# Four graph layers on one core: new issue times for every step, and the normalisation's shift on GpSimd

## The chip, the cores and the metric

One NeuronCore of a Trainium2 chip runs the program. Its engines are TensorE (PE, matrix products; PEld is its weight load), VectorE (DVE), ScalarE (ACT), GpSimd (POOL) and SyncE (SP), which issues all DMAs here. Each engine runs its own instructions strictly in the order in which the program holds them, and waits on semaphores for the others. The metric is the device time of one execution in microseconds (us); lower is better.

## The reference

64 graphs ("batches") of 256 nodes with 512 features each pass through four layers. Each layer normalises the features, and adds its result to them. All is float32.

```python
h = jnp.maximum(_layernorm(x, axis=-1), 0.0); x = x + L0(h, adj)   # and so for L1, L2, L3
L0: q, k, v = h Wqk, h Wv;  w = softmax_n(sum_m (q k^T / 8) * adj);  w * v
L1: feats = h W (8 heads of 64);  e = leaky_relu(e_self_i + e_neigh_j) masked by A;  relu(softmax(e) feats)
L2: Xp = h Wp; Xc = Xp C^T;  relu(tanh(A * Xc Xp^T) Xp)   (8 heads of 64)
L3: q, k, v = h Wqk, h Wv;  w = softmax_n(sum(q * (adj (k mask))) / sqrt(512));  w * v
```

The layer norm is (x - mean) / sqrt(var + eps), with eps = 1e-5. The kernel computes it as relu(rstd * x + shift), with rstd = (var + eps)^-0.5 and shift = -mean * rstd.

## The kernel before, in words

A batch is a graph of some 150 named steps (`graph`, a function of the kernel); each step issues a few instructions, mostly on one engine. A batch's 256 nodes lie on 128 partitions as two chunks c = 0, 1, so nearly every step works on a tile of 128 partitions by 512 columns or two of them.

The steps of one batch, in the order of the data:

- `load` (SP): x, the adjacency and its 32x32 blocks. `at`, `neg`, `negt`: the transposed adjacency and the masks made from it.
- `normed(layer)`: `st` (bn_stats and bn_aggr, DVE, L690, L692), `rs` (var + eps, DVE, L697), `pw` (power -0.5, POOL, L701), `sh` (the shift, DVE, L706), `hn` (relu(rstd x + shift), ACT, L713), then the transposition of hn into `ht`: `sq` (32x32 transposes, DVE, L645), `sw` (a write of 512 KB to DRAM, SP, L733) and `ht` (four reads back, SP, L650).
- Layer 0: `qk0`, `qk1`, `score0` (PE), `s0v` (DVE), `pv00`, `pv01`, `softp0` (PE), `softv0`, `softw0` (DVE), `softa0` (ACT), `add0` (DVE, L775).
- Layer 1: `fa`, `fb` (features, PE), `fae`, `fbe` (DVE), `send` (DVE), `er` and `enes` (SP: the score rows to DRAM and back to all partitions, 2 MB), `max0` to `max3` (DVE, L896: row maxima), `mxv`, `mxt` (DVE), `mr`, `mb` (SP: the maxima to DRAM and back to all partitions, 1 MB), `ea` (ACT, L935), `eg` (POOL, L942), `eb` (DVE, L948), `ex` (ACT, L954), each for four pairs of heads; `po` (PE, L966), `eh` (POOL, L975: sums over the two chunks), `su`, `sp` (PE), `oe`, `se` (ACT), `sr` (DVE), `sqo`, `swo`, `or` (back through DRAM), `oa0`, `oa1` (POOL, L1032, L1034).
- Layer 2: `xp` (PE), `xe` (DVE), `sqx`, `swx`, `xpt` (through DRAM), `xc` (PE), `xcv`, `xca` (ACT), `ps` (PE, L1097), `tv` (DVE, L1129), `ta` (ACT, L1136), `py` (PE, L1111), `ye` (ACT), `sqy`, `swy`, `yr`, then `yg` (POOL) and `yv` (DVE) add it to x.
- Layer 3: `am` (ACT), `agg` (PE, L1168), `ga` (ACT), `z` (PE), `zv` (DVE), `softp3`, `pv30`, `pv31` (PE), `softv3`, `softa3`, `softw3`, `add3`, `store`.

Matrix products with the full array (fa, fb, qk, pv, xp, z) share the helper `rows` and its line L639; `ps` uses 64 rows of the array, `po` and `py` 64 columns, `su` 32 columns.

**What sets the order.** The tables at the top give every step of a batch a time: `TIMES` for a batch in the steady state, `FIRST` for the first batches (6 of them), `LAST` for the last (5), `WEIGHTS` for the preparation of the weights. `Plan.sequence` adds b * `PERIOD` to the times of batch b and sorts all 9640 steps. The times are only keys: what they set is the order of the instructions on each engine.

```python
steps += [(b * PERIOD + at, b, name) for name, at in times.items()]
return sorted(steps)
```

`Plan.run` issues the steps in this order and ties each instruction to the one before it on its engine, so no scheduler moves them. Some four to five batches are under way at a time. Buffers come from pools in the order of the sequence (`take`, `done`): 8 PSUM banks, 5 `xt`, 3 `ht`, 4 `pair`, 3 `all`, 2 `half`, 2 `sq`, 2 `hn` among them; who takes a buffer waits for the last use of it.

In the steady state the order on four of the queues, from one `pv31` or `add3` to the next (the number in brackets tells batches apart, larger is later), is:

```
PE   pv31(0) qk1(4) qk0(4) pv01(4) score0(4) fb1(3) softp0(4) xp0(2) xp1(2) pv00(4) agg1(1) fb0(3) agg0(1) po2(3) z0(1)
     po0(3) xc(2) po1(3) po3(3) ps0(2) su0(3) fa0(4) fa1(4) su1(3) ps1(2) sp(3) z1(1) py0(2) softp3(1) py1(2) pv30(1)
DVE  add3(0) sh3(1) fbe1(3) xe0(2) softv0(4) sq3(1) xe1(2) sqx(2) softw0(4) eb2(3) add0(4) st1(4) rs1(4) fbe0(3) sh1(4)
     eb0(3) sq1(4) eb1(3) eb3(3) at(5) st0(5) rs0(5) zv0(1) sh0(5) sqo(3) sq0(5) fae0(4) tv1(2) fae1(4) send(4) tv0(2) ...
POOL eh0(0) eh1(0) pw0(2) eh2(0) eh3(0) oa1(0) oa0(0) pw2(0) yg(-1) pw3(-1) eg0(1) eg2(1) eg1(1) pw1(2) eg3(1)
SP   store(0) sw3(1) swx(2) ht3(1) xpt(2) load(5) sw1(4) ht1(4) swo(3) or(3) sw0(5) er(4) enes(4) ht0(5) swy(2) sw2(3) ...
```

Of the kernel before, what the change touches and what calls it, by code (L numbers as in the profile page):

```python
# [9 lines left out]
F32 = mybir.dt.float32  # L10
AF = mybir.ActivationFunctionType
OP = mybir.AluOpType
# [4 lines left out]
P = 128  # L17
# [3 lines left out]
NC = N // P  # L21
# [14 lines left out]
PERIOD = 57.0  # L36
TIMES = {
    "load": 0.000, "at": 0.020, "st0": 0.021, "rs0": 0.040, "pw0": 0.060, "sh0": 0.447, "hn0": 0.467, "sq0": 4.046,
    "neg": 5.196, "sw0": 7.794, "ht0": 17.081, "negt": 24.877, "qk1": 25.097, "qk0": 25.928, "qe0": 26.481,
    "pv01": 26.487, "qe1": 26.501, "score0": 26.521, "s0v": 30.777, "softp0": 30.797, "softv0": 37.191,  # L40
    "softa0": 37.211, "pv00": 41.031, "softw0": 42.595, "add0": 46.118, "st1": 47.198, "rs1": 47.218,
    "pw1": 47.238, "sh1": 48.461, "hn1": 49.969, "sq1": 51.679, "sw1": 57.622, "ht1": 58.705, "fa0": 58.725,
    "fae0": 61.292, "fa1": 62.955, "fae1": 64.080, "send": 64.100, "er": 65.670, "enes": 67.047, "max0": 78.054,
    "max1": 78.465, "max2": 80.041, "ea2": 81.782, "max3": 81.811, "ea0": 82.877, "mxv": 86.226, "fb1": 87.694,
    "mxt": 89.120, "mr": 89.140, "fbe1": 92.928, "mb": 92.952, "ea1": 93.137, "eg0": 97.342, "eg2": 97.898,
    "eb2": 99.758, "fb0": 101.023, "eg1": 102.751, "ex2": 103.007, "fbe0": 104.462, "ea3": 105.281, "eb0": 106.770,
    "po2": 107.965, "ex0": 109.416, "eg3": 110.046, "po0": 110.200, "eb1": 110.242, "ex1": 110.262, "po1": 112.122,
    "eb3": 112.539, "ex3": 112.559, "eh0": 112.721, "po3": 113.362, "eh1": 113.725, "oe0": 113.726, "oe1": 113.772,
    "su0": 114.984, "sqo": 116.823, "swo": 116.843, "or": 116.985, "eh2": 121.455, "eh3": 121.545, "su1": 121.565,
    "se": 121.585, "sp": 124.333, "sr": 124.353, "oa1": 127.236, "oa0": 130.191, "st2": 132.579, "rs2": 132.599,  # L50
    "pw2": 132.619, "sh2": 133.501, "hn2": 135.131, "sq2": 135.151, "sw2": 137.255, "ht2": 140.479, "xp0": 146.490,
    "xp1": 148.494, "xe0": 150.546, "xe1": 153.892, "sqx": 155.064, "swx": 156.419, "xpt": 157.903, "xc": 167.559,
    "xcv": 170.132, "ps0": 171.632, "tv1": 175.365, "xca": 177.302, "ps1": 179.802, "ta1": 179.832, "tv0": 180.487,
    "tv2": 182.563, "ta0": 182.818, "py0": 182.838, "ta2": 182.910, "tv3": 184.557, "ta3": 184.577, "am": 184.723,
    "ye0": 185.950, "py1": 187.683, "ye1": 187.703, "sqy": 190.038, "swy": 190.249, "yr": 195.049, "yv": 200.772,
    "yg": 202.748, "st3": 203.788, "rs3": 205.029, "pw3": 205.049, "sh3": 206.251, "hn3": 206.271, "sq3": 210.021,
    "sw3": 210.041, "agg1": 212.553, "ht3": 213.760, "agg0": 218.026, "ga0": 222.008, "z0": 223.305,
    "zv0": 228.215, "ga1": 230.586, "z1": 239.253, "zv1": 242.471, "softp3": 243.288, "pv30": 245.126,
    "pv31": 252.572, "softv3": 255.150, "softa3": 256.059, "softw3": 260.763, "add3": 262.405, "store": 266.901,
# [3 lines left out]
    "wn0": 268.900, "wqk": 269.000, "mt0": 269.100, "mv0": 270.100, "mm0": 270.300, "wn1": 270.400, "mt1": 271.100,  # L63
    "wv0": 271.800, "wa": 271.900, "w11": 272.400, "mv1": 272.700, "sa1": 273.100, "b2": 273.400, "mk": 273.900,
    "wn2": 274.000, "mm1": 274.100, "c2": 274.700, "b1": 274.800, "w10": 275.100, "w13": 275.200, "mt2": 275.300,
    "mv2": 275.400, "w12": 275.700, "sa3": 276.000, "sa0": 276.200, "sa2": 276.800, "mm2": 276.900, "mkp": 278.000,
    "wn3": 278.300, "mt3": 278.900, "mv3": 279.000, "mm3": 279.600, "w21": 279.900, "w22": 281.300, "ma": 281.400,
    "room": 282.600, "w20": 284.300, "mkv": 289.600, "w23": 291.300, "wv3": 295.000,
# [3 lines left out]
        "load": 268.200, "st0": 268.300, "rs0": 268.400, "pw0": 268.500, "at": 268.600, "neg": 268.700,  # L72
        "sh0": 269.200, "hn0": 269.600, "sq0": 269.700, "sw0": 269.800, "ht0": 271.300, "negt": 271.600,
        "qk0": 271.700, "qe0": 272.000, "qk1": 272.100, "qe1": 272.200, "score0": 272.300, "s0v": 272.600,
        "pv00": 273.000, "softp0": 273.200, "softv0": 273.300, "pv01": 273.500, "softa0": 273.600,
        "softw0": 273.700, "add0": 273.800, "st1": 274.200, "rs1": 274.300, "pw1": 274.400, "sh1": 274.500,
        "hn1": 274.600, "sq1": 275.500, "sw1": 276.300, "ht1": 276.500, "fa0": 277.200, "fae0": 277.400,
        "fa1": 277.500, "fae1": 277.600, "send": 277.900, "er": 278.700, "enes": 278.800, "fb0": 279.100,
        "ea2": 279.400, "ea1": 279.500, "fbe0": 280.300, "max0": 280.500, "max1": 280.700, "max3": 280.900,
        "max2": 281.000, "eg1": 281.200, "ea3": 281.600, "ea0": 281.700, "mxv": 281.800, "fb1": 281.900,  # L80
        "fbe1": 282.300, "mxt": 282.400, "eg2": 282.700, "mr": 283.400, "eg3": 283.500, "mb": 283.700,
        "eg0": 284.200, "eb0": 284.800, "eb2": 284.900, "ex0": 285.000, "eb1": 285.100, "po0": 285.200,
        "ex2": 285.300, "eb3": 285.400, "ex1": 285.500, "po2": 285.600, "po1": 285.700, "ex3": 285.800,
        "po3": 285.900, "eh1": 286.100, "eh0": 286.200, "oe0": 286.500, "oe1": 286.600, "su0": 286.800,
        "sqo": 287.200, "swo": 287.300, "or": 287.700, "eh3": 288.000, "eh2": 288.100, "su1": 288.200,
        "se": 288.600, "sp": 288.700, "sr": 288.800, "oa0": 289.700, "oa1": 289.900, "st2": 290.300,
        "rs2": 290.500, "pw2": 290.600, "sh2": 290.700, "hn2": 290.900, "sq2": 291.400, "sw2": 291.800,
        "ht2": 291.900, "xp0": 292.900, "xe0": 293.700, "xp1": 293.900, "xe1": 294.800, "sqx": 294.900,
        "swx": 295.300, "xpt": 295.500, "xc": 297.600, "xcv": 297.800, "xca": 298.200, "ps0": 298.600,
        "tv1": 299.200, "tv0": 299.300, "ta1": 299.700, "ta0": 299.800, "ps1": 299.900, "py0": 300.100,  # L90
        "tv2": 300.200, "tv3": 300.300, "ta2": 300.400, "ta3": 300.500, "ye0": 300.700, "py1": 301.000,
        "ye1": 301.100, "sqy": 301.600, "swy": 304.500, "yr": 304.700, "yg": 304.800, "yv": 305.300,
        "st3": 305.400, "rs3": 306.000, "pw3": 306.100, "sh3": 306.300, "am": 306.700, "hn3": 309.400,
        "sq3": 310.200, "sw3": 310.800, "agg1": 311.300, "agg0": 311.800, "ht3": 312.700, "ga0": 312.900,
        "ga1": 313.200, "z0": 313.800, "zv0": 315.600, "z1": 315.900, "pv31": 316.200, "zv1": 317.100,
        "softp3": 317.200, "pv30": 317.600, "softv3": 318.000, "softa3": 318.400, "softw3": 318.500,
        "add3": 319.000, "store": 319.100,
    },
    {
        "load": 212.500, "st0": 213.200, "rs0": 213.500, "pw0": 213.600, "sh0": 213.700, "hn0": 213.800,  # L100
        "at": 213.900, "sq0": 214.400, "neg": 215.800, "sw0": 215.900, "ht0": 217.900, "qk0": 218.600,
        "qk1": 218.800, "qe0": 218.900, "pv00": 219.100, "qe1": 219.400, "score0": 219.600, "s0v": 219.700,
        "softp0": 220.100, "softv0": 220.300, "softa0": 220.700, "pv01": 220.800, "softw0": 221.100,
        "add0": 221.200, "st1": 221.400, "rs1": 221.500, "pw1": 221.600, "sh1": 222.200, "hn1": 222.300,
        "sq1": 223.000, "sw1": 223.200, "ht1": 224.500, "fa0": 225.200, "fb0": 225.800, "fae0": 225.900,
        "fa1": 226.100, "fbe0": 226.200, "fae1": 229.300, "fb1": 229.400, "send": 229.700, "er": 230.000,
        "negt": 230.600, "enes": 232.800, "ea0": 233.000, "ea2": 233.400, "max0": 233.800, "max2": 234.600,
        "max3": 235.000, "ea3": 235.100, "ea1": 235.200, "max1": 235.300, "mxv": 235.400, "mxt": 235.800,
# [328 lines left out]
def tile_four_gnn_layers(ctx: ExitStack, tc: tile.TileContext, x, adj, nodemask,  # L437
# [48 lines left out]
    far = consts.tile([P, 1], F32)  # L486
    nc.gpsimd.memset(far, NEG_BIG)
    power = consts.tile([P, NC], F32)
    nc.gpsimd.memset(power, -0.5)
    for t in plan.pools["mx"]:  # L490
        nc.gpsimd.memset(t, 0.0)

# [742 lines left out]
```

## Time and profile before

| | us |
|---|---|
| the runs of the kernel | 3867.55, 3868.8, 3875.89 (median 3868.8) |
| the profiled execution, span from the first instruction to the last | 3876.7 |
| PE busy in that span | 3717.5 |
| DVE busy | 3178.4 |
| ACT busy | 1893.0 |
| POOL busy | 1576.0 |

The page gives no time of the profiled execution other than its span. Busy times are sums over an engine's instructions. A row of the timeline has the start in the span, the length, the engine, the line and operation, what it writes and reads (out<-in), the shape and the number of instructions merged into it; brackets at its end give the idle time of the engine before it and who ended that. A float32 matrix product appears as two instructions, and the recorded lengths of PE overlap: the spacing of the starts tells how fast it goes. In the chain of waits each row is a piece of the path that ended last: start, length, what. The row of one line gives the shortest, the median and the longest of its instructions in ns.

### The profile page before, as it was taken

What the parts mean: (1) busy time and instruction counts of PE and PEld (TensorE: products, weight loads), DVE (VectorE), ACT (ScalarE), POOL (GpSimd) and SP (SyncE); (2) the same over time, 40 slices, a digit from 0 to 9 for tenths busy, and PEclk for the clock granted to TensorE, in tenths of its full rate; (3) what the DMA queues carried; (4) which work ended last, traced back from release to release, by engine and by line L of the source; (5) the groups of instructions that cost most, each with busy time, mean ns of one, the idle gap of its engine ahead of it and who ended that gap; (6) DMA issues with size and microseconds to landing.
All of it is one profiled execution on the core that took longest, in us unless ns stands there. A gap on an engine that the chain in (4) does not pass through costs nothing.

```text
span 3876.7 us, 53433 instructions
## 1 busy us (share of the span) xinstructions
PE 3717.5 (96%) x16322; PEld 2105.0 (54%) x16322; DVE 3178.4 (82%) x7449; ACT 1893.0 (49%) x3653; POOL 1576.0 (41%) x1229
## 2 busy tenths in 40 slices
PE   7799999999999999999999999999999999999889
PEld 4455555555555555555555555555555555555544
DVE  6787888888888888788888888888888888887774
ACT  2454454455454454454554544544544544545442
POOL 1443444444444444343344344444444444443441
PEclk9899999999999999999999999999999999999999
DMA  7666677777676676666667767766766776776653
GB/s 198 199 200 199 201 212 205 207 212 207 209 216 202 208 214 202 196 205 209 204 201 212 213 202 208 211 199 203 218 201 212 208 203 209 213 202 202 183 174 114
DMA packets 967439, 784.76 MB, mean 202 GB/s; under 512 B 788912, under 2 KB 859120, under 8 KB 942576
## 3 DMA queue, kind: packets, MB, share of 16 engines
q1 hardware_dynamic: 967152, 781.34, 67.6%
q8 instruction: 131, 2.15, 0.2%
q14 instruction: 156, 1.28, 0.1%
HBM read 511.12 MB, written 270.01 MB: 201 GB/s over the span
## 4 chain that ended last, share of the span: by engine, by line
PE 57%; DVE 14%; DMA 10%; issue 6%; SPq 6%; ACT 4%; POOL 3%; DVEq 0%; POOLq 0%; ACTq 0%
PE bank L639 39%; PE bank L1111 6%; SPq L650 5%; DMA ht<-sq_d 4%; DMA sq_d<-sq 4%; PE bank L1097 4%; DVE shift L706 3%; PE bank L966 3%; DVE sq L645 2%; DVE junk L896 2%; POOL pair L942 2%; ACT hn L713 2%; PE bank L1075 1%; DVE stats L690 1%; PE bank L821 1%
## 5 line engine op out<-in xcount | busy, mean ns | idle before, releaser
L639 PE MATMUL bank<-w_s,ht 128*128 128x256 f32 (+2 forms) x3072 | 964.2, 465 | 88.1 <-DMA ht<-sq_d 70.8
L639 PE MATMUL bank<-wv_s,ht 128*128 128x512 f32 x2048 | 919.5, 596 | 1.8 <-ACT qk L811 1.7
L639 PEld LDWEIGHTS bank<-w_s,ht 128*128 128x128 f32 x3072 | 598.6, 200 | 407.5 <-issue 263.7
L713 ACT ACTIVATE hn<-xt,shift,rstd 128x512 f32<-128x512 f32 x512 | 388.7, 807 | 786.4 <-DVE shift L706 767.1
L942 POOL TENSOR_TENSOR pair<-pair,negt 128x1024 f32<-128x1024 f32 x256 | 607.3, 2384 | 121.5 <-ACT pair L935 121.5
L639 PEld LDWEIGHTS bank<-wv_s,ht 128*128 128x128 f32 x2048 | 392.2, 196 | 440.5 <-issue 436.6
L975 POOL TENSOR_TENSOR half<-pair 128x512 f32<-128x512 f32 x256 | 388.8, 1531 | 325.5 <-ACT pair L954 198.3
L701 POOL TENSOR_TENSOR rstd<-rstd,power 128x2 f32<-128x2 f32 x256 | 179.6, 702 | 787.8 <-DVE rstd L697 786.8
L896 DVE CUSTOM_DVE_ANT_0 junk<-all,adj 128x256 f32<-128x256 f32 x1024 | 460.5, 450 | 31.0
L639 PE MATMUL bank<-m_s,ht 128*128 128x512 f32 x1024 | 466.8, 599 | 5.3 <-DMA ht<-sq_d 3.9
L935 ACT ACTIVATE pair<-all,ec 128x256 f32<-128x256 f32 x1024 | 431.8, 494 | 17.7 <-DMA all<-er_d 17.7
L954 ACT ACTIVATE pair<-pair 128x1024 f32<-128x1024 f32 x256 | 269.7, 1057 | 327.6 <-DVE pair L948 326.9
L690 DVE BATCH_NORM_STATS2 stats<-xt 128x6 f32<-128x512 f32 x512 | 325.8, 677 | 77.3 <-POOL xt L1034 68.6
L948 DVE TENSOR_TENSOR pair<-pair,all 128x1024 f32<-128x1024 f32 x256 | 365.9, 1451 | 3.0 <-DMA all<-m_d 2.8
L1149 POOL TENSOR_TENSOR xt<-xt,hn 128x512 f32<-128x512 f32 x64 | 90.7, 1417 | 653.7 <-DMA hn<-sq_d 653.7
L645 DVE STREAM_TRANSPOSE sq<-hn 128x512 f32<-128x512 f32 x512 | 331.9, 685 | 9.3 <-ACT hn L713 9.1
L1136 ACT ACTIVATE pair<-pair 128x512 f32<-128x512 f32 x512 | 295.2, 626 | 74.8 <-DVE pair L1129 74.8
L1129 DVE TENSOR_TENSOR pair<-bank,at 128x512 f32<-128x512 f32 x512 | 317.5, 673 | 16.3 <-PE bank L1097 16.2
L639 PEld LDWEIGHTS bank<-m_s,ht 128*128 128x128 f32 x1024 | 192.5, 197 | 213.9 <-issue 211.2
L1032 POOL TENSOR_TENSOR hn<-hn,rs 128x256 f32<-128x256 f32 x256 | 152.2, 616 | 368.1 <-DVE rs L1020 202.0
L966 PE MATMUL bank<-pair,feats 128*64 128x256 f32 x2048 | 271.8, 399 | 25.5 <-ACT pair L954 19.0
L706 DVE SCALAR_TENSOR_TENSOR shift<-mv,rstd 128x2 f32<-128x2 f32 x256 | 257.2, 1005 | 47.1 <-POOL rstd L701 42.9
(83 smaller groups left out, 4405.6 us busy)
## 6 DMA issues: line engine op xcount, KB each, us to landing
sq_d<-sq SPq DMA_DIRECT2D x448, 512.0 KB
ht<-sq_d SPq DMA_DIRECT2D x1024, 128.0 KB
all<-er_d SPq DMA_DIRECT2D x128, 1024.0 KB
all<-m_d SPq DMA_DIRECT2D x64, 1024.0 KB
hn<-sq_d SPq DMA_DIRECT2D x512, 128.0 KB
xt<-in_x_dram SPq DMA_DIRECT2D x64, 512.0 KB
xpt<-sq_d SPq DMA_DIRECT2D x256, 128.0 KB
out_dram<-xt SPq DMA_DIRECT2D x64, 512.0 KB
```

The lines of the kernel that those rows point to most:

```text
L639: nc.tensor.matmul(p, chunk(ht[:, k], c), w[:, k], start=(k == 0), stop=(k == KC - 1))
L645: nc.vector.transpose(sq.rearrange("p (r k i c) -> p c k r i", r=4, k=KC, c=NC)[:, c], t[:, c])
L690: nc.vector.bn_stats(stats[:, c, :], g["xt"][:, c, :])
L706: nc.vector.scalar_tensor_tensor(st["shift"], st["mv"][:, :, 0], -1.0, st["rstd"], op0=OP.mult, op1=OP.mult)
L713: nc.scalar.activation(hn[:, c, :], g["xt"][:, c, :], AF.Relu, bias=st["shift"][:, c:c + 1], scale=st["rstd"][:, c:c + 1])
L896: nc.vector.tensor_tensor_reduce(junk, g["en"][:, h, :], g["adj"][:, c, :], 1.0, -BIG, OP.add, OP.max, g["mx"][:, c, h:h + 1])
L935: nc.scalar.activation(e[:, s, j, :], g["es"][:, h, :], AF.Prelu, bias=st["ec"][:, j, H + h:H + h + 1], alpha=0.2)
L942: nc.gpsimd.tensor_tensor(e, e, g["negt"][:, None].to_broadcast([P, 2, NC, N]), OP.add)
L948: nc.vector.tensor_tensor(e, e, g["m"][:, 2 * p:2 * p + 2, None, :].to_broadcast([P, 2, NC, N]), OP.subtract)
L966: nc.tensor.matmul(po[s * U:(s + 1) * U, p % 2, :], feats[:, j, h * U:(h + 1) * U], e[:, s, j, :], start=(j == 0), stop=(j == NC - 1))
L975: nc.gpsimd.tensor_tensor(g.take("half", name=f"h{p}"), e[:, :, 0, :], e[:, :, 1, :], OP.add)
L1129: nc.vector.tensor_tensor(th[:, s], g[f"ps{p}{s}"].rearrange("p (m n) -> p m n", m=NC), g["at"], OP.mult)
```

## The change

All four tables get new values, and PERIOD goes from 57.0 to 56.5; nine batches have times of their own at the start (six before) and eight at the end (five). The steps and their contents stay the same, except for `sh`, which moves from one DVE instruction to two products on POOL, the second by a constant of -1.0 that is set once at the start.

```diff
-PERIOD = 57.0
+PERIOD = 56.5
 TIMES = {
-    "load": 0.000, "at": 0.020, "st0": 0.021, "rs0": 0.040, "pw0": 0.060, "sh0": 0.447, "hn0": 0.467, "sq0": 4.046,
...
+    "load": -22.128, "st0": -17.398, "rs0": -15.679, "pw0": -8.012, "at": -4.693, "sh0": -1.337, "hn0": -1.317,
...
+    "max2": 70.314, "mxv": 70.457, "mxt": 70.758, "fbe0": 71.839, "ea3": 72.079, "fbe1": 72.983, "eg2": 73.744,
+    "mr": 73.753, "mb": 73.773, "eb2": 77.427, "eg3": 77.510, "ea0": 77.623, "ex2": 78.776, "eg0": 80.458,
+    "eb0": 82.433, "eb1": 82.550, "ex1": 82.570, "ex0": 86.179, "eh1": 86.899, "eh0": 87.814, "su0": 87.925,
...
     power = consts.tile([P, NC], F32)
     nc.gpsimd.memset(power, -0.5)
+    minus = consts.tile([P, NC], F32)
+    nc.gpsimd.memset(minus, -1.0)
...
             @step(f"sh{layer}")
             def _():
                 st["shift"] = small.tile([P, NC], F32, name="shift")
-                nc.vector.scalar_tensor_tensor(st["shift"], st["mv"][:, :, 0], -1.0, st["rstd"],
-                                               op0=OP.mult, op1=OP.mult)
+                nc.gpsimd.tensor_tensor(st["shift"], st["mv"][:, :, 0], st["rstd"], OP.mult)
+                nc.gpsimd.tensor_tensor(st["shift"], st["shift"], minus, OP.mult)
```

Sorted by the new times, the steady order on the queues is (DVE and POOL shown in full, as they carry the move of `sh`):

```
PE   pv31(0) fb0(3) pv30(0) pv01(4) qk0(4) qk1(4) xp0(2) xp1(2) score0(4) agg0(1) softp0(4) pv00(4) agg1(1) z0(1) su0(3)
     po2(3) po0(3) po1(3) xc(2) po3(3) su1(3) ps0(2) ps1(2) sp(3) fa0(4) fa1(4) z1(1) py1(2) py0(2) fb1(4) softp3(1)
DVE  add3(0) sq3(1) xe0(2) eb2(3) xe1(2) s0v(4) sqx(2) softv0(4) eb0(3) eb1(3) softw0(4) add0(4) st1(4) rs1(4) eb3(3)
     sq1(4) zv0(1) st0(5) sqo(3) rs0(5) tv1(2) tv0(2) tv2(2) tv3(2) fae0(4) at(5) fae1(4) send(4) sr(3) sq0(5) zv1(1)
     st2(3) rs2(3) sqy(2) sq2(3) softv3(1) max0(4) max3(4) max1(4) max2(4) mxv(4) mxt(4) yv(2) st3(2) rs3(2) fbe0(4)
     fbe1(4) softw3(1)
POOL eh0(0) pw1(1) sh1(1) eh2(0) eh3(0) pw0(2) sh0(2) oa0(0) oa1(0) pw2(0) sh2(0) eg1(1) yg(-1) pw3(-1) sh3(-1) eg2(1)
     eg3(1) eg0(1) eh1(1)
SP   store(0) ht3(1) swx(2) load(5) xpt(2) sw1(4) ht1(4) swo(3) or(3) er(4) sw0(5) enes(4) swy(2) ht0(5) sw2(3) yr(2)
     ht2(3) mr(4) mb(4) sw3(2)
```

## Prediction

> **What bounds the kernel now.** I read the page's busy shares and slices first, then the waits, then one batch of TensorE (PE) in the timeline, then the chain of waits over that stretch. The page:
>
> ```profile
> span 3876.7 us, 53433 instructions
> PE 3717.5 (96%) x16322; PEld 2105.0 (54%) x16322; DVE 3178.4 (82%) x7449; ACT 1893.0 (49%) x3653; POOL 1576.0 (41%) x1229
> PE   7799999999999999999999999999999999999889
> ```
>
> PE is busy nearly everywhere; only the first two slices and the last four fall off. What fills PE shows in its timeline, start by start:
>
> ```profile
> 2405.58 1.95 PE L639 MATMUL bank<-w_s,ht 128*128 128x256 f32 x8
> 2407.37 0.38 PE L751 MATMUL bank<-ident,wc 128*128 128x128 f32 x2
> 2407.59 7.04 PE L639 MATMUL bank<-w_s,ht 128*128 128x512 f32 x16
> ...
> 2417.90 1.88 PE L1168 MATMUL bank<-hn,at 128*128 128x512 f32 x4
> 2419.61 1.89 PE L639 MATMUL bank<-w_s,ht 128*128 128x256 f32 x8
> 2421.34 1.88 PE L1168 MATMUL bank<-hn,at 128*128 128x512 f32 x4
> 2423.15 1.08 PE L966 MATMUL bank<-pair,feats 128*64 128x256 f32 x8
> ...
> 2434.82 0.64 PE L989 MATMUL bank<-half,ones 128*32 128x256 f32 x8
> 2437.07 3.91 PE L639 MATMUL bank<-w_s,ht 128*128 128x272 f32 x16 [1.61 <-DMA ht<-sq_d]
> ...
> 2447.30 1.95 PE L1111 MATMUL bank<-pair,xp 128*64 128x256 f32 x16
> 2449.18 0.43 PE L751 MATMUL bank<-ident,wc 128*128 128x128 f32 x2
> 2449.54 1.95 PE L1111 MATMUL bank<-pair,xp 128*64 128x256 f32 x16
> ```
>
> Two things stand here. First, PE runs back to back, and a change of array shape (128\*128, 128\*64, 64\*128, 128\*32) costs about 0.1 us on either side of it: the adjacency step L1168 takes 1.71 us ahead of a full-shape step (2417.90 to 2419.61) and 1.81 ahead of L966 (2421.34 to 2423.15); the little transpose L751 takes 0.22 between full-shape steps and 0.36 between two L1111. Second, one wait per batch is real: the layer-1 features (fa0) wait for ht1. The chain of waits names what is late there:
>
> ```profile
> 2408.63 1.31 DVE xt L775 x2
> 2409.94 1.82 DVE shift L706
> 2411.84 1.22 ACT hn L713 x2
> ...
> 2426.11 1.24 DVE sq L645 x2
> 2427.36 4.83 DMA sq_d<-sq
> 2434.17 2.77 DMA ht<-sq_d
> 2437.07 3.91 PE bank L639 x16
> ```
>
> The 1.82 us there is a product of 2 columns. The row of L706 has its shortest, median and longest:
>
> ```profile
> L706 DVE SCALAR_TENSOR_TENSOR shift<-mv,rstd x256: 108/162/2302, 7.3 to 3843.1; 128x2 f32<-128x2 f32 x128
> ```
>
> So its work is 0.11 us and the rest is waiting inside the instruction, in places where POOL is in a long product (sh1 averages 2.30 over batches 14 to 49, sh3 1.88, sh0 and sh2 0.16 and 0.12).
>
> **The sum of before.** I gave every PE step its usual shortest spacing to the next one, by the shapes of its neighbours, as all rows of the trace show it. In the steady order that is 57.07 us a batch; the batches come every 58.65 us (st0 of batch 14 to st0 of batch 50, over 36). The 1.56 us between are waits, 1.23 of them at fa0. Over the whole span the spacings make 3663.7, so 213 us are lost: 90 by batch 8, 78 in the steady part (52 batches), 45 at the end. I work against this execution; its span of 3876.7 is 7.9 above the median of the runs, 3868.8, and I take 8 off at the end. The page gives no other time of it.
>
> **The change, part by part.**
>
> *The order on PE.* Sorted by the new times, one batch of PE is: pv31 fb0 pv30 pv01 qk0 qk1 xp0 xp1 score0 agg0 softp0 pv00 agg1 z0, su0, po2 po0 po1, xc, po3, su1, ps0 ps1, sp fa0 fa1 z1, py1 py0, fb1 softp3. It has 9 changes of shape for 15 (588 for 926 in the program). The same spacings give 56.02 us a batch, 1.05 less, and 3605.7 in all, 58.0 less. No work is added or taken on PE.
>
> *The shift.* DVE loses 257.2 us / 64 = 4.02 us a batch, nearly all of it waiting. POOL gets two 2-column products per normalisation, each behind a wait on POOL itself. No row shows one: from below, a POOL memset of 2 columns takes 0.10; from above, pow on the same shape takes 0.70. I take 0.15, near the memset since the pow's length is its function, and 0.08 for the wait (L1032 to L1034 in the timeline): 0.46 a shift, bounds 0.36 and 1.56. POOL goes from 24.6 to 26.5 us of the batch, so its time is free; what is queued behind it counts, and that is in the loop below. The new constant is one memset at the start, about 0.1 us.
>
> A page of the Trainium skill speaks against this move. "GPSIMD Engine Reference", section 4.1 (Engine selection), sends elementwise products to VectorE because GpSimd is about twice slower with two inputs. The row above shows VectorE at 0.16 to 2.30 us here, so the rule counts arithmetic where this row counts waiting. By the rule the shift alone would be a loss of some tenths of a us per layer, by the row a gain of up to 1.8 at two of the four.
>
> *The loop that the order makes.* In before, fa0's lateness hangs on xp1 of the same batch slot: xp1 ends, xe1, sqx, softw0, eb2, add0, st1, rs1, pw1, sh1, hn1, sq1, DMA, fa0, 22.1 us against 20.9 of PE work between. In the new order ps0 and ps1 stand together and fa0 comes behind both: PE has 22.3 between xp1 and fa0, and DVE meets eb0 and eb1 ahead of add0. But eb2 now stands ahead of xe1, s0v and sqx, and eb2 needs the row maxima of the same batch, which come from its own fa. That closes a loop through one batch, and I add it up with before's means (us): fa0, fa1, fae1, send 4.55; er until enes is issued 3.9; its last 8 KB packet 7.0 later, with sq2 and softv3 in the way, max0 at 15.9; four max 7.35; mxv, mxt 1.75; mr until mb is issued 2.65; mb's last packet and its signal 5.7 (33.35 so far); eb2, xe1, s0v, sqx, softv0, eb0, eb1 7.55; ex1, then eh1 and eh0 on POOL, 4.3, because pw1 now stands behind them (by softw0, add0, st1, rs1 it would be 3.6); pw1 and the shift 1.3; hn1 and sq1 2.4; sq_d written until ht1 is issued 3.2 to 4.1 (3.09 is sw2's mean, 4.10 sw1's, which shares with the loads of 1 MB that now come earlier); four issues 2.6; landing 2.45. Together 57.2 to 58.1. I take 57.7 and 0.15 for uneven batches: **57.85** a batch where it was 58.65.
>
> The PE sum of 56.02 lies under that, so the waiting grows from 1.56 to 1.8 us, and of the 1.05 that the shapes give 0.8 stays; what is late next is eb2 (through s0v and softp0) and ht1. Also moved past each other: on SP, load now stands ahead of xpt, and sw1 behind both; swx to xpt is 3.5, four issues 2.6, landing 2.5, which has xpt there about 1 us ahead of xc. PSUM is full while ps0 and ps1 run (8 banks); ps1 needs xca and se, which by the rows end 0.3 to 1 us ahead of it. These are thin covers; without them about 0.5 us a batch each.
>
> *The ends.* First and last batches get their own times, nine and eight of them for six and five. The shapes give 3.4 us there. The latency of one batch (185 us from pv00 to the end for batch 63) stays; 157 us of PE work follow that batch's qk0 for 183 before, so the tail can't shrink much. Bounds from the losses of 90 and 45: 30 gained, 30 lost. I take 10 gained, no more, since the first stalls (fa0, po0, fa of batch 2) have the same sources in both orders.
>
> Sum: 52 x (58.65 - 57.85) = 42, ends 13, so 3876.7 - 55 = 3822 of span, less 8: **3814 us**.
>
> **Rivals.** (1) *The loop is shorter than I think*, PE is the bound: 56.2 to 56.6 a batch, 52 x 2.25 = 117, with the ends 130: 3739 to 3755. For it: DVE is 4 us freer, so sq2, max and eb2 may come earlier. Against it: er, enes, mr and mb are DMA time, 19 us of the loop. (2) *POOL's queue turns the loop slower.* pw1 stands behind eh0 and eh1, and eb0 and eb1 on DVE run beside products of POOL. The rows have such pairs: eh1 2.14 where eh2 takes 1.27, eb3 2.30 where eb2 takes 1.22. With eb0, eb1 and both eh at the long form the loop gets 1.1 x 2 + 0.6 x 2 = 3.4 longer, 61.2 a batch: 3814 + 175 = 3989; with one of each, 59.5: 3900. It decides from 0.9 us above my 57.85 on. (3) *The waits eat the shapes whole*, 58.4 to 58.8 a batch and ends alike: 3868, no change.
>
> **Chances.** Forecast (57 to 58.3 a batch) 0.56, rival 1 0.19, rival 2 0.18, rival 3 0.07. Measuring this kernel tells 0.2%, 8 us, from no change. Faster 0.75, within 0.07, slower 0.18. The range leaves out half of each far case: 3748 to 3890.
>
> **What would show it.** Right: PE's time per batch about 57.8 with a [<-] at fa0 or at softp0 of 1 to 2 us; the shape changes fewer, so L751 at 0.22; L706's place taken by two POOL products of 0.1 to 0.2; eb2 waiting for all<-m_d, which before cost 2.8 us in the whole run. Wrong: batches under 57, or eb2 never waiting (rival 1); pair L975 means of 2 us and hn waiting for POOL shift (rival 2); lost time at the ends beyond 30 us either way.

## The result and the profile after

The changed kernel takes 3976.4 us (median of 4 runs, 3971.7 to 3992.9), the kernel before 3868.7 beside it (3867.6 to 3875.9): **2.8% slower**, ratio 1.0283, 95% interval 1.0261 to 1.0305. The forecast was 3814. The page of the profiled execution:

```profile
span 3972.9 us, 53445 instructions
PE 3706.7 (93%) x16322; PEld 2124.4 (53%) x16322; DVE 3156.0 (79%) x7193; ACT 1857.8 (47%) x3653; POOL 1708.3 (43%) x1742
```

PE's share falls from 96% to 93%: it waits more. (The clock is no rival for this: the records show PE at half clock for 91 us, before for 79, which is worth at most 6 us of PE's time, an estimate: half of the difference.) The sum of the prediction can be made again on this trace. With each PE step at its usual spacing, the new order needs 3605.7 us, as forecast, 58 under the old one. The time lost beyond that is 367 us where it was 213: 96 by batch 8 (90 before), 206 from there to batch 60 (78), 65 behind it (45). So -58 + 6 + 128 + 20 = +96, which is the difference of the spans. A batch comes every 59.78 us (fa0 of batch 14 to fa0 of batch 50, over 36), and 3.76 of these are waits of PE, 1.56 before.

One batch of PE in the timeline, in which three of these waits stand in brackets:

```profile
1870.17 1.16 PE L982 MATMUL bank<-qk,at 128*128 128x64 f32 x8 [0.77 <-ACT qk L972]
1873.73 0.73 PE L912 MATMUL bank<-ident,wc 128*128 128x128 f32 x2 [0.62 <-DVE bank L990]
1895.24 0.93 PE L800 MATMUL bank<-w_s,ht 128*128 128x272 f32 x3 [1.28 <-DMA ht<-sq_d]
```

They are score0 (waits for qe1 on ACT), softp0 (waits for s0v on DVE) and fa0 (waits for ht1). What is late ahead of them shows in the chain of waits of the same batch (start, length, what):

```profile
1852.51 0.43 DVE junk L1057
1852.98 2.45 DVE junk L1057
...
1859.68 1.37 DVE junk L1057
...
1864.99 4.89 DMA all<-m_d
...
1869.98 1.42 DVE pair L1109
1871.39 1.41 issue
```

L1057 is a piece of a row maximum (L896 before). Fourteen of the sixteen pieces of this batch take 0.42 us; one takes 2.45 and one 1.37, and the chain shows nothing that they wait for. eb2 (L1109, L948 before) then takes 2.9 us, which the chain parts into 1.42 and an "issue" of 1.41, where an eb on its own takes 1.22. POOL's timeline of these microseconds tells why:

```profile
1852.62 2.53 POOL L1103 TENSOR_TENSOR pair<-pair,negt 128x1024 f32<-128x1024 f32 x1 [4.03 <-ACT pair L1096]
1859.21 1.55 POOL L1310 TENSOR_TENSOR xt<-xt,hn 128x512 f32<-128x512 f32 x1 [4.07 <-DMA hn<-sq_d]
...
1869.44 2.35 POOL L1103 TENSOR_TENSOR pair<-pair,negt 128x1024 f32<-128x1024 f32 x1 [0.90 <-ACT pair L1096]
1871.97 3.14 POOL L1103 TENSOR_TENSOR pair<-pair,negt 128x1024 f32<-128x1024 f32 x1 [0.17 <-ACT pair L1096]
...
1882.42 1.60 POOL L862 TENSOR_TENSOR rstd<-rstd,power 128x2 f32<-128x2 f32 x1
```

eg1 runs from 1852.62 to 1855.15: the long piece begins in it and ends at 1855.43, 0.3 us behind eg1's end. The second long one ends 0.3 us behind yg (L1310). eb2 begins while eg3 runs (1869.44 to 1871.79) and ends 1.1 us behind it, as if it had begun there; then eg0, which begins at 1871.97, takes 3.14 us in place of 2.35, for it waits for eb2's end. pw1 takes 1.60 at 1882.42, because eb3 (1.21 us from 1882.25) runs. So **such an instruction of DVE and one of POOL stand in each other's way, for the whole of the instruction that is under way** (which instructions of DVE do, is listed at the end). Over the whole trace, a piece of a maximum takes 0.42 us alone and 1.25 to 1.33 in the mean beside a POOL instruction; some 258 of 1024 lie so, 32 in the kernel before. The group's line before, and then in the changed kernel, with that of eb behind it:

```profile
L896 DVE CUSTOM_DVE_ANT_0 junk<-all,adj 128x256 f32<-128x256 f32 x1024 | 460.5, 450 | 31.0
```

```profile
L1057 DVE CUSTOM_DVE_ANT_0 junk<-all,adj 128x256 f32<-128x256 f32 x1024 | 646.8, 632 | 32.9 <-DMA all<-er_d 0.2
L1109 DVE TENSOR_TENSOR pair<-pair,all 128x1024 f32<-128x1024 f32 x256 | 393.0, 1562 | 38.1 <-DMA all<-m_d 35.7
```

The 257 us that DVE spent in L706 are gone, but 186 of them came back in the maxima, 27 in eb (365.9 to 393.0) and some 20 in others: DVE's busy time falls by 22 us only. The shift itself is what was forecast, two products of 0.2 us:

```profile
L867 POOL TENSOR_TENSOR shift<-mv,rstd x256: 188/194/653, 6.8 to 3941.8; 128x2 f32<-128x2 f32 x128
```

### The profile page after: what moved, and what is told of

Read it like the earlier page. It is cut to its first block, busy times and chain, and to the rows that moved or that the text cites. A ratio compares the mean times of both kernels' runs of the same rounds, so it can differ in the third digit from the quotient of the medians.

```text
span 3972.9 us, 53445 instructions
## 1 busy us (share of the span) xinstructions
PE 3706.7 (93%) x16322; PEld 2124.4 (53%) x16322; DVE 3156.0 (79%) x7193; ACT 1857.8 (47%) x3653; POOL 1708.3 (43%) x1742
## 4 chain that ended last, share of the span: by engine, by line
DVE 36%; PE 22%; DMA 20%; POOL 9%; issue 6%; SPq 5%; ACT 3%; DVEq 0%; POOLq 0%; ACTq 0%
DVE junk L1057 15%; PE bank L800 10%; DMA all<-m_d 5%; DVE sq L806 5%; DMA hn<-sq_d 4%; PE bank L1127 3%; POOL xt L1195 3%; DVE pair L1109 3%; DMA sq_d<-sq 3%; POOL hn L1193 3%; DMA adj<-in_adj_dram 3%; PE bank L1236 3%; PE bank L1258 2%; DVE stats L851 2%; DVE pair L1290 2%
## 5 line engine op out<-in xcount | busy, mean ns | idle before, releaser
L1103 POOL TENSOR_TENSOR pair<-pair,negt 128x1024 f32<-128x1024 f32 x256 | 654.9, 2563 | 352.4 <-ACT pair L1096 328.1
L1057 DVE CUSTOM_DVE_ANT_0 junk<-all,adj 128x256 f32<-128x256 f32 x1024 | 646.8, 632 | 32.9 <-DMA all<-er_d 0.2
L862 POOL TENSOR_TENSOR rstd<-rstd,power 128x2 f32<-128x2 f32 x256 | 222.7, 870 | 653.9 <-DVE rstd L858 607.7
L1136 POOL TENSOR_TENSOR half<-pair 128x512 f32<-128x512 f32 x256 | 333.0, 1312 | 378.0 <-ACT pair L1115 350.5
L806 DVE STREAM_TRANSPOSE sq<-hn 128x512 f32<-128x512 f32 x512 | 346.1, 698 | 185.7 <-ACT hn L874 183.3
L1109 DVE TENSOR_TENSOR pair<-pair,all 128x1024 f32<-128x1024 f32 x256 | 393.0, 1562 | 38.1 <-DMA all<-m_d 35.7
L1297 ACT ACTIVATE pair<-pair 128x512 f32<-128x512 f32 x512 | 284.7, 620 | 249.2 <-DVE pair L1290 249.0
L1127 PE MATMUL bank<-pair,feats 128*64 128x256 f32 x2048 | 253.6, 390 | 34.4 <-ACT pair L1115 32.1
L1329 PE MATMUL bank<-hn,at 128*128 128x512 f32 x512 | 243.2, 599 | 3.3 <-ACT hn L874 3.3
L1258 PE MATMUL bank<-xc,xpt 64*128 64x256 f32 x2048 | 242.3, 384 | 3.9 <-ACT xc L1244 3.8
```

What stands on the lines that cost most here:

```text
L806: nc.vector.transpose(sq.rearrange("p (r k i c) -> p c k r i", r=4, k=KC, c=NC)[:, c], t[:, c])
L1057: nc.vector.tensor_tensor_reduce(junk, g["en"][:, h, :], g["adj"][:, c, :], 1.0, -BIG, OP.add, OP.max, g["mx"][:, c, h:h + 1])
L1103: nc.gpsimd.tensor_tensor(e, e, g["negt"][:, None].to_broadcast([P, 2, NC, N]), OP.add)
L1109: nc.vector.tensor_tensor(e, e, g["m"][:, 2 * p:2 * p + 2, None, :].to_broadcast([P, 2, NC, N]), OP.subtract)
L1127: nc.tensor.matmul(po[s * U:(s + 1) * U, p % 2, :], feats[:, j, h * U:(h + 1) * U], e[:, s, j, :], start=(j == 0), stop=(j == NC - 1))
L1136: nc.gpsimd.tensor_tensor(g.take("half", name=f"h{p}"), e[:, :, 0, :], e[:, :, 1, :], OP.add)
```

## The experiments

Each ran with the kernel before on the same chip (3875 to 3880 us there). The theory under test, A: the maxima and eb2 are long because of POOL's products (so its long TENSOR_TENSOR instructions are called here, eg above all, though eg and yg add), and they lie in the loop from fa0 to the next fa0. Each expectation below sets A against a rival, B or C. Means per step are over batches 14 to 49.

**The two halves of the change apart.** `order_only` has the new tables with the shift on DVE as it was, `shift_only` the old tables with the shift on POOL.

The diff is that of the first, against the changed kernel; the second is its reverse in the kernel before, with the constant `minus`.

```diff
-                nc.gpsimd.tensor_tensor(st["shift"], st["mv"][:, :, 0], st["rstd"], OP.mult)
-                nc.gpsimd.tensor_tensor(st["shift"], st["shift"], minus, OP.mult)
+                nc.vector.scalar_tensor_tensor(st["shift"], st["mv"][:, :, 0], -1.0, st["rstd"],
+                                               op0=OP.mult, op1=OP.mult)
```

> The changed kernel with its new times, but the shift back as one DVE instruction. Theory A (the new order closes a loop through fa0, the row maxima, mb, eb2 and ht1, and in it DVE's products of two SBUF operands stand still while POOL runs one): the cost lies in the order, so this stays slow; sh1 and sh3 stall again beside POOL, sh1 lies in the loop: 3976 to 4040. Rival B (the two products on POOL, queued behind other POOL work, are what costs): back to 3870 or less.

Measured 4086.5 us, ratio 1.0536 (1.0498 to 1.0573): slow, as A had it, and B falls, but the loss is larger than A's range. The new order alone costs 5.4%, and within it the shift on POOL gives back 106 us of span (4078.9 to 3972.9). Of the two shifts that were to stall only sh3 does: it takes 2.29 us on DVE there and 0.39 on POOL; sh1 takes 0.16 on DVE.

> The kernel before with its own times, only the shift moved to two products on POOL. Theory A: no loop is closed, sh1 shrinks from 2.30 us on DVE to about 0.5 on POOL, fa0's wait of 1.23 us a batch goes and about 0.3 to 0.5 is left to other waits: 3790 to 3830, faster than before. Rival B: 3880 to 3980, slower than before. If other DVE instructions take over the standing still: 3850 to 3870.

Measured 3912.0, ratio 1.0087 (1.0055 to 1.0118): a loss of 0.9%, and A a miss. The time lies in B's range, but the products on POOL are not what is slow: sh1 does fall from 2.30 to 0.85 us, and sq1 ends 1.4 us earlier behind the last xp1. From sq1's end to fa0, though, it is now 11.1 us for 9.2, and SP has this in its queue ahead of ht1:

```profile
1798.98 0.62 SPq L663 DMA_DIRECT2D xt<-in_x_dram  x1
1799.64 0.43 SPq L664 DMA_DIRECT2D adj<-in_adj_dram  x1
1800.11 1.91 SPq L668 DMA_DIRECT2D blocks<-in_adj_dram  x4
1802.12 0.40 SPq L735 DMA_DIRECT2D sq_d<-sq  x1
1808.10 2.54 SPq L652 DMA_DIRECT2D ht<-sq_d  x4
```

sw1 (1802.12) now stands at the end of a closed row of issues, the load's six right ahead of it: from sq1's end to sw1's issue 1.08 us in the mean for 0.09 before, and from sw1 to ht1 4.81 for 4.10, with the load's 1 MB on its way. The gain ends there. Part of the rest goes with the granted clock of PE: the profiled execution, whose span is 50 us longer than before, has 135 us at half clock for 79, which is up to 28 us of PE time (an estimate: half of the difference).

**One product made small.** `eg1_small` is the changed kernel with eg1 (the one beside the maxima) on 2 of 256 columns; the rest of that mask is left out.

```diff
-                nc.gpsimd.tensor_tensor(e, e, g["negt"][:, None].to_broadcast([P, 2, NC, N]), OP.add)
+                if p == 1:
+                    nc.gpsimd.tensor_tensor(e[:, :, :, :2], e[:, :, :, :2],
+                                            g["negt"][:, None, :, :2].to_broadcast([P, 2, NC, 2]), OP.add)
+                else:
+                    nc.gpsimd.tensor_tensor(e, e, g["negt"][:, None].to_broadcast([P, 2, NC, N]), OP.add)
```

> The changed kernel, in which the mask of the second pair of heads (eg1) is added to 2 columns of each 256 only, so that POOL's product of 2.5 us beside max3 shrinks to some 0.1 us; the rest of that mask is left out. Theory A: max3 falls from 3.94 to about 2.0 us, and since max lies in the loop the batch gets about 1.5 us shorter: 3976 - 52 x 1.5 = 3898, between 3870 and 3930. Rival C (fa0 is late because of the work between xp1 and fa0 alone, the maxima are off the path): 3960 to 3980.

Measured 3864.6, ratio 0.9951 (0.9935 to 0.9967): 118 us less span than the changed kernel, by 2 us of work a batch taken from an engine that is busy 43% of the time. The line of the maxima:

```profile
L1057 DVE CUSTOM_DVE_ANT_0 junk<-all,adj 128x256 f32<-128x256 f32 x1024 | 476.0, 465 | 33.4 <-DMA all<-er_d 0.7
```

All four maxima take 2.02 us, a batch 57.87, though eb2 (2.80) and pw1 (1.61) are as long as in the changed kernel. That is somewhat more than theory A gave it, and far from C. It also shortens the ends, since its edit holds in all batches: fa0 of batch 8 comes 14.8 us earlier than in the changed kernel, and the stretch behind fa0 of batch 60 is 9.5 us shorter.

**Two products put beside the maxima, in the kernel before.** The reverse, without any work added or left out: `eg_beside` moves eg2 and eg0 ahead of yg.

```diff
-    "mxt": 89.120, "mr": 89.140, "fbe1": 92.928, "mb": 92.952, "ea1": 93.137, "eg0": 97.342, "eg2": 97.898,
+    "mxt": 89.120, "mr": 89.140, "fbe1": 92.928, "mb": 92.952, "ea1": 93.137, "eg0": 83.0, "eg2": 82.9,
```

> The kernel before, with two of POOL's four mask products (eg2, eg0) put ahead of yg in the steady batches, so that they run where DVE runs the maxima; no work is added or left out. Theory A: a maximum, having two inputs in SBUF, and a product of POOL exclude each other, so the four maxima grow from 7.4 us by about 2 us for each product, to 11 or 12, and DVE, which works nearly without a gap from the maxima to rs1, passes 2 to 4 us of it on to the batch: 3960 to 4050. Rival B: the maxima are long in the changed kernel for another reason (their place behind softv3, the transfer that feeds them): they stay at 7.4 us here and the time within 20 us of the kernel before.

Measured 4095.7, ratio 1.0567 (1.0544 to 1.0589), more than A gave it. The timeline of DVE, and then of POOL:

```profile
1906.31 2.60 DVE L896 CUSTOM_DVE_ANT_0 junk<-all,adj 128x256 f32<-128x256 f32 x1
1908.95 2.45 DVE L896 CUSTOM_DVE_ANT_0 junk<-all,adj 128x256 f32<-128x256 f32 x1
1911.44 0.42 DVE L896 CUSTOM_DVE_ANT_0 junk<-all,adj 128x256 f32<-128x256 f32 x1
1911.91 1.39 DVE L896 CUSTOM_DVE_ANT_0 junk<-all,adj 128x256 f32<-128x256 f32 x1
```

```profile
1906.27 4.85 POOL L942 TENSOR_TENSOR pair<-pair,negt 128x1024 f32<-128x1024 f32 x2 [4.91 <-ACT pair L935]
1911.75 1.27 POOL L1149 TENSOR_TENSOR xt<-xt,hn 128x512 f32<-128x512 f32 x1 [0.63 <-DMA hn<-sq_d]
```

Two products of 2.4 us, two maxima of 2.5 us; yg's 1.27, one of 1.39. The four maxima sum to 13.2 us for 8.1 (max1 6.19, max2 2.99), a batch is 62.72 for 58.63. Rival B, that something else makes the maxima long, falls. That the place of POOL's products makes them long, and that this reaches the time, is shown both ways.

**The exits of the loop.** In the changed kernel eb2 has 2.83 us ahead of xe1, s0v and sqx, and score0 waits 1.16 us for qe1, which stands behind hn3 on ACT. `eb2_late` puts eb2 behind softv0; `qe_early` puts neg, qe0 and qe1 ahead of hn3; `eb2_qe` does both. Of the edits the changed keys alone are shown, here and below.

```diff
eb2_late, eb2_qe
-"eb2": 77.427, "ex2": 78.776
+"eb2": 80.80, "ex2": 80.81
qe_early, eb2_qe
-"neg": 15.924, "qk0": 16.917, "qk1": 17.374, "qe0": 19.927, "qe1": 19.947
+"neg": 14.302, "qk0": 14.300, "qk1": 14.301, "qe0": 14.303, "qe1": 14.304
```

> The changed kernel, but in the steady state eb2 and ex2 stand behind softv0 of the next batch, just ahead of eb0, and no longer ahead of xe1, s0v and sqx. Theory A: xe1, s0v, sqx and softv0 (4 us) leave the loop and only eb2, eb0, eb1 wait for mb; what is left is some 57.5 to 58.3 us a batch: 3860 to 3910. Rival C: the same instructions stand between xp1 and fa0 as before, so nothing changes: 3960 to 3985.

> The new order, with neg, qe0 and qe1 put ahead of hn3 on ACT (qk0, qk1 keep their place on PE). Theory A: the long maxima delay two exits of one stretch of DVE: fa0 of the next batch (through eb2, sqx, add0, rs1, sw1, ht1) and score0 (through yv, rs3, sh3, hn3, and behind hn3 qe1). Freeing score0 alone, whose wait is 1.16 us a batch, only moves PE's wait to fa0: within 20 us of the changed kernel, 3955 to 3980. Rival C: the wait at score0 is a loss of its own: 1.16 x 52 = 60 us less, about 3916.

> The new order with both edits: eb2 behind softv0 on DVE (alone it gave 18 us), and neg, qe0, qe1 ahead of hn3 on ACT. Theory A: with both exits free, the 1.6 us of eb2 leave the loop: 1.2 to 1.6 us a batch over 52, that is 62 to 83 us under the changed kernel: 3890 to 3915. Rival C: two lone effects that add up, 18 and whatever neg, qe0, qe1 give alone; if that is under 20, 3940 to 3960.

Measured 3958.7 (ratio 1.0207, 1.0179 to 1.0235), 3994.7 (1.0306, 1.0275 to 1.0336) and 3954.7 (1.0205, 1.0178 to 1.0233). The first and the third were to gain 60 us or more by theory A, and did not; both lie at or in C's range. The second lies 18 us above the changed kernel, within the 20 that A gave it but above its 3955 to 3980; the freed wait turns up at softp0, not at fa0. With both edits the wait at score0 is gone, and PE waits 1.66 us at xc and about 0.5 each at su0 and fa0 instead. The loop says why: from mxt to rs1 18.56 us for 19.59, since eb2 still takes 2.21 beside eg0, and 0.6 of that 1.0 is lost again between rs1 and fa0. DVE's queue says it too: in the changed kernel DVE is idle for only 0.83 us of the 31.1 from max0 to rs1, and eb2's wait for mb is 0.5 of these; in `eb2_qe` it is idle for 0.41. So eb2 moved back leaves DVE's own work where it was, and an exit freed gives little while the maxima themselves, 3 us too long, stay in that work; that part of A had been too hopeful.

**The products put away.** `eg_moved` is `eb2_qe` with eg2, eg1 and eg0 together behind sh3, eg3 behind sh1 and eb3 behind sq1; `eg_moved2` also puts eh2 behind eh3, and su1 and se behind ps0. Everything is computed.

```diff
eg_moved, eg_moved2
-"eg1": 70.094, "ea3": 72.079, "eg3": 77.510, "ea0": 77.623, "eg0": 80.458, "eb3": 92.207
+"eg1": 77.505, "ea3": 77.623, "eg3": 91.000, "ea0": 72.079, "eg0": 77.510, "eb3": 92.300
eg_moved2
-"eh2": 91.347, "su1": 96.317, "se": 96.877
+"eh2": 96.298, "su1": 97.183, "se": 97.200
```

> As the one before, and POOL's four mask products put where DVE runs operations that their trace shows untouched: eg2, eg1, eg0 behind sh3 (beside bn_stats, transposes and operations that read PSUM), eg3 behind sh1, eb3 behind sq1 (ea0 and ea3 change places on ACT). Everything is computed. Theory A: the four maxima go back from 10.4 to 7.4 us and the loop falls under PE's own work of 56.02 us and a wait of about 1: 3800 to 3850, under the kernel before. Rival C: the products and DVE's operations meet elsewhere and the batch stays over 58 us: 3890 or more.

Measured 3895.9, ratio 1.0052 (1.0034 to 1.0071). The maxima take 2.02 us each, pw1 0.70, eb2 1.22, but eb3 takes 2.27 us beside eh2, and PE waits 1.19 us for po3 behind it. 59 us are gained on `eb2_qe`, where A asked for over 100: the time lies in C's range, and eb3 beside eh2 is a meeting elsewhere, as C had it.

> The version with the products moved (3896), and eh2 put behind eh3 on POOL and su1 (with se) behind ps0, since in its trace eb3 took 2.24 us beside eh2 and PE waited 1.19 us for po3 behind it and 0.31 us at su1. Theory A: eb3 goes back to 1.2 us and that wait goes: 1.2 to 1.5 us a batch over 52, 62 to 78 less: 3820 to 3835, under the kernel before. Rival C: the wait turns up again at fa0 or another place of PE: 3870 to 3900.

Measured **3860.8, ratio 0.9957 (0.9939 to 0.9974)**: the new order, with POOL's products out of DVE's way, is 0.4% faster than the kernel before. A batch is 57.19 us, of it about 1.1 waits of PE. The gain on `eg_moved`, 35 us, is half of what was expected: po3's wait fell from 1.19 to 0.35, fa0's rose from 0.14 to 0.46. POOL's timeline has the three products in one row:

```profile
1811.95 7.02 POOL L1103 TENSOR_TENSOR pair<-pair,negt 128x1024 f32<-128x1024 f32 x3
```

DVE and POOL do the same work as in the changed kernel and are busy 174 and 90 us less (2981.8 and 1618.0 us). The three products lie beside bn_stats, transposes and operations that read PSUM, and take 2.34 each.

**The shift on DVE in that order.** `moved2_dve` is `eg_moved2` with the diff of `order_only`.

> The version that ran in 3861 (products and eh2 moved), with the shift back on DVE as one instruction; everything is computed. Theory A: the shift has two inputs in SBUF, so on DVE it stands still while a product runs, and behind sh3 POOL begins eg2 as soon as pw3 is done: sh3 takes 2.3 us instead of 0.4, and with it the stretch of DVE between the maxima and rs1 grows by 1.5 to 2 us a batch: 3900 to 3970. In the order before, whose queue of SP ended last, the same half of the change gained nothing (3912 for 3880). Rival B: the half that moves the shift is worth nothing in any order: 3850 to 3875.

Measured 4120.4, ratio 1.0628 (1.0587 to 1.067): 260 us for one instruction of 2 columns per normalisation, far beyond the 40 to 110 expected. DVE, then POOL:

```profile
1929.12 2.29 DVE L867 SCALAR_TENSOR_TENSOR shift<-mv,rstd 128x2 f32<-128x2 f32 x1 [0.81 <-POOL rstd L862]
```

```profile
1929.05 4.67 POOL L1103 TENSOR_TENSOR pair<-pair,negt 128x1024 f32<-128x1024 f32 x2
```

POOL begins eg2 behind pw3, 0.07 us ahead of the shift, which stands until it is done; sh1 does the same behind pw1 (2.31). A batch grows from 57.19 to 61.47. In this order the shift belongs on POOL, where nothing can get between pw and it.

**The load out of sw1's way.** The order before with the shift on POOL, and the load issued behind the store and sw3 (`shift_load`, -17.9) or between ht3 and xpt (`shift_load2`, -14.2), from batch 12 on. The part that moves the load, of the first:

```diff
+FIRST = FIRST + (TIMES,) * 6
+TIMES = dict(TIMES, load=-17.900)
```

> The order before with the shift on POOL (3912 alone), and in the steady batches the load two batches ahead issued behind the store instead of ahead of sw1. Theory A: the shift's 1.4 us at sh1 were gained, but sw1 then stood behind the load's six issues on SP and beside its 1 MB (sw1 to ht1 4.8 us for 4.1); with the load away 1.2 to 2 us a batch are gained over about 45 batches: 3800 to 3840. Rival B: what holds the batch is not SP (PE's clock windows, or another wait): 3880 to 3920.

> The order before with the shift on POOL, and the load put between ht3 and xpt, not ahead of ht3 (where z0 then waited 2.24 us for ht3, 3946 in all, though fa0's wait had gone). Theory A: neither ht3 nor sw1 now stands behind the load: 1 to 1.5 us a batch less than with the shift alone (3912): 3835 to 3865. Rival B: xpt, now 3 us later, makes xc wait, or the clock windows stay: 3890 to 3930.

Measured 3945.8 (1.0183, 1.0158 to 1.0208) and 3894.4 (1.0045, 1.0029 to 1.0061): both miss what A gave them, and the second lies in B's range, with the wait that B named. In both fa0's wait, 1.76 us with the shift alone, is nearly gone (0 and 0.10), as A had it; but in the first z0 waits 2.24 us for ht3, which now stands behind the load, in the second xc 1.40 for xpt. In each of the three places the late step is one that SP issues behind the load. So SP's queue decides there which step is late; whether by the load's six issues or by its 1 MB on the way, no run parts, and a place for the load that gains was not found.

## Why the prediction was wrong

- *PE's sum* held: 3605.7 us, 58 less, nine shape changes.
- *The loop* was the right one: fa0 to max0 was put at 15.9 us and is 16.0; mr to mb's issue 2.65, is 2.4; mb's landing 5.7, is 4.75; hn1 and sq1 2.4, are 2.3; ht1's issues and landing 5.05, are 5.1. eb2 does wait for mb, as was to be seen (35.7 us in the run for 2.8), but by 0.5 us a batch only: beside the way over mr and mb runs DVE's own queue, which the sum did not have and which is nearly as long. The maxima lie ahead of both.
- **The step that failed is "four max 7.35"**, taken from the means of before, with eg1 now beside them. It is 10.4: +3.05 us a batch. The same error in two smaller terms: "eb2, xe1, s0v, sqx, softv0, eb0, eb1 7.55" is 8.7 (eb2 2.83 for 1.22), "pw1 and the shift 1.3" is 2.3 (pw1 1.60 for 0.70). These three, +5.2, less some 3 us of terms that were sized too long, make 57.7 into 59.8. `eg1_small` shows it most plainly: with eg1 small and so the maxima short again, a batch is 57.87 us, where 57.85 were forecast. That this falls so close is luck in part, for eb2 and pw1 stay long there and make up for the terms that were too long. `eg_beside` shows the reverse, and `eg_moved2`, an order with other changes too, runs at 57.19 without these collisions.
- *Rival 2*, which I gave 0.18, had the right cause at the wrong instructions. It priced eb0, eb1, eh0 and eh1 by rows of 2.1 and 2.3 us; those stayed short (1.22 and 1.27). Its mark of 0.9 us was passed by max alone. The rows stood in the trace: L706 with 0.11 us of work and up to 2.30 of waiting. I read them as a property of the shift and used them for DVE's gain; they were a price for every such instruction that the new order would put beside a product.
- *A rule of the Trainium skill speaks to this*: "SBUF — State Buffer", section "Who interferes with whom", states that a VectorE instruction with two SBUF inputs contends with a GpSimd instruction that reads SBUF, over a pair of ports that they share, and calls this "an exclusive lock". These rows agree (a piece of a maximum 0.42 us alone, up to 2.63 beside a product; eb 1.22 and up to 3.42). I had weighed only the rule on elementwise speed.
- *The shift*: 0.46 us forecast, 0.47 found with its wait. Its worth depends on the order: +32 us in the old one, -106 in the new, -260 in the mended one.
- *The ends* were put at 13 gained, 10 of them in waits; the waits grew by 26 instead. In batches 0 to 7 the maxima stand 40 us above their 8.0 a batch, 17 before, and `eg1_small`, where these are 20, gets 14.8 us back ahead of batch 8 and 9.5 behind batch 60: so a good part of this loss has the same cause. The rest stays open.

## What to carry to other kernels

When a change moves instructions in time, list for each DVE instruction with two inputs in SBUF what POOL runs beside it, before and after; a mean from the old order holds only for its old neighbours. A row whose longest is many times its shortest (here 2.30 and 0.11 us), without a wait in front, can be the price of such a neighbour: look what POOL ran beside it, and expect the same of the other instructions of that kind. An engine that is busy 43% of the time can set the end through another engine's time, so put its long instructions beside work that the rows show untouched.

## What the runs showed of the hardware

- Which DVE instructions stand still beside POOL: those with two SBUF inputs (a piece of a maximum 0.42 us alone and up to 2.63, eb 1.22 and up to 3.42, the shift 0.11 and up to 2.30, yv 0.69 and up to 2.8) and TENSOR_SCALAR (L930 in `moved2_dve`: about 1.5 us beside a product, 0.23 alone). Untouched: those with an input in PSUM (add0 and add3, L775: 0.74 us alone and beside), bn_stats (0.68 us alone and beside in the changed kernel) and the 32x32 transposes (sq3 0.69 and 0.70).
- It holds both ways: POOL's pow takes 0.70 us, and 1.60 where eb3 is under way; eg0 3.05 for 2.35.
- PE's granted clock falls to half for 3.41 us or a multiple of it, mostly behind a wait of PE of over 2 us. In batches 14 to 49 of the fourteen traces, 88 of 104 such pieces begin within 9 us behind one; 85 of 149 such waits are followed by a piece. Half-clock time was 79 us before, 91 in the changed kernel, 135 in `shift_only`, 209 in `eg_beside`, 214 in `moved2_dve`. A piece of 3.41 us costs up to 1.7 us of PE's time, an estimate: half of its length.
